# Products of zeros in TensorE's waits, and an earlier second tile, at the start of an RWKV block

## The chip, the cores and the metric

The kernel runs on one core of a Trainium2 chip. The metric is the device time of one execution in microseconds (us); lower is better. The engines of a core are TensorE (PE, matrix products into PSUM), VectorE (DVE), ScalarE (ACT), GpSimd (POOL) and SyncE (SP). Each has its own instruction stream, taken in order, and they wait for each other through semaphores. DMA transfers are issued from the queues of SP, ACT and POOL.

## The reference

The input is x with shape (2, 4096, 256). Two residual sublayers follow each other, both behind a layer normalisation without weights:

```python
x = x + attn(_layernorm(x))
x = x + ffn(_layernorm(x))
# attn: xk, xv, xr = mixes of x and x shifted by one in time
k = xk @ W_k.T;  v = xv @ W_v.T;  r = sigmoid(xr @ W_r.T)
# WKV, a scan over time with a running maximum p and numerator q
new_p = maximum(p, u + k_t)
wkv_t = (exp(p - new_p) * q + exp(u + k_t - new_p) * v_t) / (exp(p - new_p) + exp(u + k_t - new_p))
p, q  = maximum(p + w, k_t), exp(p + w - p2) * q + exp(k_t - p2) * v_t     # p2: the new p
attn = (r * wkv) @ W_o.T
# ffn, weights of -1, 0 and 1 with a scale per output
h = silu(x @ w1.T * s1) * (x @ w2.T * s2)        # 256 -> 1024
h = gelu(h @ h1.T * sh1);  h = gelu(h @ h2.T * sh2)
ffn = h @ w3.T * s3                              # 1024 -> 256
```

## The kernel before, in words

Features lie on partitions (two halves of 128, `ND` = 2), time on the free axis. Time is cut into 16 tiles of `TS` = 512 columns, 8 for each of the two sequences. Tile 0 alone is worked in two parts of 256 columns (`parts`, line 86), so that its engines can overlap, since nothing else is there to run beside it.

Every step is a generator that yields between groups of instructions: `normalise(i)` (line 260) makes the first layer normalisation, `attention(i)` (275) the mixes, the products k, v, r (`ps_k`, `ps_v`, `ps_r`, line 300), the scan (`wkv`, 204), the output product (`ps_o`, 312), the residual and the second normalisation (`layernorm`, 176), and `ffn(i)` (335) the feed-forward part. The driver at lines 387 to 402 runs tile 0's normalisation and attention, then tile 1's normalisation, and then the feed-forward of each tile with the attention of the next and the normalisation of the one after it mixed in. A scheduler then orders the instructions of each engine by priority and readiness, so the order on an engine is not simply the order of the source. A pool of buffers hands out tiles, and a new tile waits until the old one in its buffer has been read.

A layer normalisation takes the mean with a product: VectorE adds the two halves (`both`, line 182), TensorE multiplies by a matrix of 1/256 (`average`, line 167; `mean`), VectorE subtracts, ScalarE squares (line 192), VectorE adds the halves (193), TensorE multiplies again (`var`), ScalarE takes the root (196), VectorE the reciprocal (199) and the product (201). In tile 0 the averages are f32 products (line 174); in later tiles the operand is first split in a high and a low half of type fp32r (`split`, line 162; `sums`) and the product made of two.

In the feed-forward part each product is made of a high and a low half (`split_product`, line 154; lines 159 and 160 in the profile): `pa` and `pb` (first layer), `ph` (the two hidden layers), `po` (last). `pa` goes through Silu on ScalarE (`gated`, line 346), is multiplied by `pb` on VectorE (line 347) and split (`hi`, `lo`). ScalarE loads a table of functions when the kind of function changes (`ACT_TABLE_LOAD`).

PSUM pools: `ps_attn` has three buffers, `ps_sum` one, `ps_ffn` four. x is loaded on SP's and ACT's queue for tile 0 (line 93) and on POOL's for all others. POOL's queue also carries, ahead of tile 1's load, the weights w1, w2 and h1, eight copies of h2 within HBM (`h_hbm`, line 112) and w3.

Of the kernel before, what the change touches and what calls it, by code (L numbers as in the profile page):

```python
# [7 lines left out]
F32 = mybir.dt.float32  # L8
# [54 lines left out]
def split_block(ctx, tc, flags, x, vecs, w_attn, w1, w2, h1, h2, w3, out):  # L63
# [26 lines left out]

    def load_x(i):
        x_sb = xpool.tile([P, ND, TS], F32, tag="x", name="x_sb")
        for p, queue in zip(parts(i), (nc.sync, nc.scalar) if i == 0 else (nc.gpsimd,)):
            queue.dma_start(out=x_sb[:, :, p], in_=hbm(x, *tiles[i])[:, :, p])
        return x_sb

    loaded = {0: load_x(0)}
    vec = const.tile([P, NVEC], F32, name="vec")
    nc.sync.dma_start(out=vec, in_=vecs)
    wa_sb = const.tile([P, 4, ND, D], F32, name="wa_sb")  # L100
# [11 lines left out]
        nc.gpsimd.dma_start(out=h2_hbm[f], in_=h2[:, :, f * P : (f + 1) * P])  # L112
    nc.gpsimd.dma_start(out=w3_sb, in_=w3)

    mean_w = const.tile([P, P], F32, name="mean_w")
# [3 lines left out]
    eps = const.tile([P, 1], F32, name="eps")  # L119
    vector.memset(eps, LN_EPS)  # L120
    unmix = const.tile([P, 3 * ND], F32, name="unmix")
    vector.tensor_scalar(unmix, vec[:, 0 : 3 * ND], -1.0, 1.0, ALU.mult, ALU.add)

    prev = const.tile([P, ND, 1], F32, name="prev")
    log_max = const.tile([P, ND], F32, name="log_max")
    numer = const.tile([P, ND], F32, name="numer")


    pieces = []
# [24 lines left out]
    def split_product(psum, weights, src):  # L154

        n = len(src)
        for c in range(n):
            hi, lo = src[c]
            tensor.matmul(psum, weights(c), hi, start=c == 0, stop=False)  # L159
            tensor.matmul(psum, weights(c), lo, start=False, stop=c == n - 1)  # L160

    def split(hi, lo, full):

        scalar.activation(hi, full, AF.Copy)  # L164
        vector.tensor_tensor(lo, full, hi.bitcast(F32), ALU.subtract)  # L165

    def average(psum, both, busy):

        if busy:
            pieces = one.tile([P, 2, TS], F32R, tag="sums", name="sums")  # L170
            split(pieces[:, 0, :], pieces[:, 1, :], both)
            split_product(psum, lambda c: mean_wr, [(pieces[:, 0, :], pieces[:, 1, :])])
        else:
            tensor.matmul(psum, mean_w, both, start=True, stop=True)

    def layernorm(src, xc, tag, parts, busy):


        both = one.tile([P, TS], F32, tag=tag, name="both")
        mean = ps_sum.tile([P, TS], F32, tag="ps", name="mean")  # L180
        for p in parts:
            vector.tensor_tensor(both[:, p], src[:, 0, p], src[:, 1, p], ALU.add)
            average(mean[:, p], both[:, p], busy)
        for p in parts:
            for h in range(ND):
                vector.tensor_tensor(xc[:, h, p], src[:, h, p], mean[:, p], ALU.subtract)
        yield
        sq = wide.tile([P, ND, TS], F32, tag="wide", name="sq")
        var = ps_sum.tile([P, TS], F32, tag="ps", name="var")
        rstd = one.tile([P, TS], F32, tag=tag, name="rstd")  # L190
        for p in parts:
            scalar.activation(sq[:, :, p], xc[:, :, p], AF.Square)
            vector.tensor_tensor(sq[:, 0, p], sq[:, 0, p], sq[:, 1, p], ALU.add)
            average(var[:, p], sq[:, 0, p], busy)
        for p in parts:
            scalar.activation(rstd[:, p], var[:, p], AF.Sqrt, bias=eps)  # L196
        yield
        for p in parts:
            vector.reciprocal(rstd[:, p], rstd[:, p])  # L199
            for h in range(ND):  # L200
                vector.tensor_tensor(xc[:, h, p], xc[:, h, p], rstd[:, p], ALU.mult)
        yield

    def wkv(h, k, v, r, y, parts, first):

        w, u = col(DECAY, h), col(FIRST, h)

        lm = one.tile([P, TS + 1], F32, tag="lm", name="lm")
        num = one.tile([P, TS + 1], F32, tag="num", name="num")
        if first:  # L210
            vector.memset(lm[:, 0:1], LOG_ZERO)
# [14 lines left out]
        for p in parts:  # L226
            vector.tensor_tensor_scan(
                lm[:, after(p)], w.to_broadcast([P, p.stop - p.start]), k[:, p], lm[:, p.start : p.start + 1],
                ALU.add, ALU.max,
            )  # L230
            vector.scalar_tensor_tensor(sc[:, 1, p], lm[:, p], w, k[:, p], ALU.add, ALU.subtract)
            vector.tensor_scalar(sc[:, 0, p], sc[:, 1, p], NEG_CLAMP, 0.0, ALU.max, ALU.min)
            vector.tensor_scalar(sc[:, 1, p], sc[:, 1, p], 0.0, -NEG_CLAMP, ALU.max, ALU.min)
            scalar.activation(sc[:, 0, p], sc[:, 0, p], AF.Exp)
            scalar.activation(sc[:, 1, p], sc[:, 1, p], AF.Exp, scale=-1.0)
            vector.scalar_tensor_tensor(so[:, 1, p], k[:, p], u, lm[:, p], ALU.add, ALU.subtract)
            vector.tensor_scalar(so[:, 1, p], so[:, 1, p], NEG_CLAMP, -NEG_CLAMP, ALU.max, ALU.min)
        vector.tensor_copy(log_max[:, h : h + 1], lm[:, TS:])
        for p in parts:
            scalar.activation(so[:, 0, p], so[:, 1, p], AF.Sigmoid, scale=-1.0)  # L240
            scalar.activation(so[:, 1, p], so[:, 1, p], AF.Sigmoid)
            scalar.activation(r[:, p], r[:, p], AF.Sigmoid)
        yield
        for p in parts:
            vector.tensor_tensor(sc[:, 1, p], sc[:, 1, p], v[:, p], ALU.mult)
            vector.tensor_tensor_scan(
                num[:, after(p)], sc[:, 0, p], sc[:, 1, p], num[:, p.start : p.start + 1], ALU.mult, ALU.add
            )
        vector.tensor_copy(numer[:, h : h + 1], num[:, TS:])
        yield  # L250
        for p in parts:
            vector.tensor_tensor(so[:, 0, p], so[:, 0, p], num[:, p], ALU.mult)
            vector.tensor_tensor(so[:, 1, p], so[:, 1, p], v[:, p], ALU.mult)
            vector.tensor_tensor(so[:, 0, p], so[:, 0, p], so[:, 1, p], ALU.add)
            vector.tensor_tensor(y[:, h, p], so[:, 0, p], r[:, p], ALU.mult)
        yield
# [3 lines left out]
    def normalise(i):  # L260

        x_sb = loaded.pop(i)
        if i + 1 < len(tiles):
# [7 lines left out]
        yield from layernorm(x_sb, xn[:, :, 1:], "rstd1", parts(i), i > 0)  # L271
        vector.tensor_copy(prev, xn[:, :, TS:])
        normal[i] = (x_sb, xn)

    def attention(i):
# [21 lines left out]
        for h in range(ND):  # L297
            kvr = []
            for m, name in enumerate("kvr"):
                ps = ps_attn.tile([P, TS], F32, tag="pa", name="ps_" + name)  # L300
                for p in ps_of:
                    product(
                        ps[:, p],
                        lambda c, m=m: wa_sb[:, m, c, h * P : (h + 1) * P],
                        [mixed[m][:, c, p] for c in range(ND)],
                    )
                kvr.append(ps)
            yield
            yield from wkv(h, *kvr, y, ps_of, first)

        for h in range(ND):
            ps = ps_attn.tile([P, TS], F32, tag="pa", name="ps_o")
            for p in ps_of:
# [4 lines left out]
                )  # L318
                vector.tensor_tensor(x_sb[:, h, p], x_sb[:, h, p], ps[:, p], ALU.add)
        yield  # L320
        x2 = wide.tile([P, ND, TS], F32, tag="wide", name="x2")
        yield from layernorm(x_sb, x2, "rstd2", ps_of, i > 0)
# [60 lines left out]
    def run(steps):  # L383
        for _ in steps:
            pass

    normal, got = {}, {}
    run(normalise(0))
    run(attention(0))
    run(normalise(1))  # L390
    for i in range(len(tiles)):
        ahead = attention(i + 1) if i + 1 < len(tiles) else iter(())
        further = normalise(i + 2) if i + 2 < len(tiles) else iter(())
        for step, _ in enumerate(ffn(i, *got.pop(i))):

            if step >= NH:
                next(ahead, None)
            if step > 2 * NH - 2 and step % 2:
                next(further, None)
        run(ahead)  # L400
# [288 lines left out]
```

## Time and profile before

| What | us |
|---|---|
| median of 3 runs | 1613.53 (1613.01 to 1614.44) |
| the profiled execution, its own time | 1613.69 |
| its span, first to last instruction | 1611.9 |
| TensorE busy | 1571.8 |
| VectorE, ScalarE busy | 1077.4, 1014.0 |
| first `mean` product of tile 0 | 5.10 |
| first `ps_k` product | 16.85 |
| first `pa` product | 57.74 |
| first `ph` product | 77.65 |

A row of a timeline has the start in us, the time, the engine, the line, the operation, the tile written and the tiles read, the shape, the count, and in brackets the idle time before it with what ended it. f32 products of 128x256 show as two records each, so "x8" is four products. Matmuls are pipelined: of several in a row, the start-to-start distance is the cost. A row of windows has the busy time and the number of instructions of PE, PE's weight loads (PEld), DVE, ACT and POOL, then the clock granted to TensorE, the DMA share and GB/s. The mean granted clock of the core over the span is 0.993. DMA queue q10 is ACT's, q1 is SP's and q0 POOL's.

### The profile page before, as it was taken

The page shows a single profiled execution, that of the slowest core. Times are in us where ns is not written, and L with a number is a line of the kernel's source. Part 1 is how long each engine was busy: PE and PEld are TensorE (multiplying, and loading weights), DVE is VectorE, ACT ScalarE, POOL GpSimd, SP SyncE. Part 2 cuts the span into 40 slices and gives each one's busy share as a digit, 9 for nine tenths or more (in the row PEclk, how much of TensorE's full clock was granted, in tenths as well). Part 3 has the DMA queues.
Part 4 walks back from the last instruction along what each step waited for, and adds up shares of the span by engine and source line. Part 5 has one row for each costly group of instructions (what it writes and reads, how often), then busy time and mean ns, then how long its engine had stood idle before and what let it go on. Part 6 is the DMA issues. An engine that isn't in the chain of part 4 may idle for free.

```text
span 1611.9 us, 16567 instructions
## 1 busy us (share of the span) xinstructions
PE 1571.8 (98%) x6314; PEld 1189.0 (74%) x6314; DVE 1077.4 (67%) x1746; ACT 1014.0 (63%) x1351; POOL 58.4 (4%) x91
## 2 busy tenths in 40 slices
PE   4799999999999999999999999999999999999997
PEld 3577778777777777777777777777778777787786
DVE  7767667585766958668585676857668575675521
ACT  6566666766657567576666657667576666657542
POOL 2000000000000000000000000000000000000000
PEclk9899999999999999999999999999999999999999
DMA  9003122130311203113030221203112031110202
GB/s 366 26 1 105 40 79 72 33 116 15 105 53 53 92 14 118 39 52 99 19 119 27 78 72 43 96 13 102 43 53 85 7 105 40 65 59 34 91 9 72
DMA packets 36230, 109.16 MB, mean 68 GB/s; under 512 B 3632, under 2 KB 12336, under 8 KB 35504
## 3 DMA queue, kind: packets, MB, share of 16 engines
q1 hardware_dynamic: 18992, 68.45, 13.0%
q0 software_dynamic: 16880, 39.33, 7.9%
q8 instruction: 51, 0.84, 0.2%
q14 instruction: 35, 0.29, 0.1%
q10 hardware_dynamic: 272, 0.26, 0.0%
HBM read 99.64 MB, written 12.58 MB: 70 GB/s over the span
## 4 chain that ended last, share of the span: by engine, by line
PE 79%; issue 15%; DMA 3%; DVE 1%; ACT 1%; POOL 0%; POOLq 0%; ACTq 0%
PE ph L159 24%; PE ph L160 24%; PE pa L159 3%; PE pa L160 3%; PE pb L159 3%; PE pb L160 3%; PE po L159 3%; PE po L160 3%; PE ps_o L152 3%; PE ps_v L152 3%; PE ps_r L152 3%; PE ps_k L152 3%; DMA h_hbm<-in_h 1%; DMA x_sb<-in_x 1%; PE mean L159 0%
## 5 line engine op out<-in xcount | busy, mean ns | idle before, releaser
L159 PE MATMUL ph<-hi,h_sb 128*128 128x512 f32 x2048 | 817.2, 399 | 0.3 <-DMA h_sb<-h_hbm 0.3
L160 PE MATMUL ph<-lo,h_sb 128*128 128x512 f32 x2048 | 803.7, 393 | 0.0
L159 PEld LDWEIGHTS ph<-hi,h_sb 128*128 128x128 f32 x2048 | 384.6, 188 | 95.4 <-issue 7.4
L160 PEld LDWEIGHTS ph<-lo,h_sb 128*128 128x128 f32 x2048 | 385.0, 188 | 90.8 <-issue 7.2
L365 DVE TENSOR_TENSOR lo<-full,hi 128x512 fp32r<-128x512 f32 x256 | 175.3, 685 | 321.7 <-ACT full L364 321.6
L362 ACT ACTIVATE hi<-ph,vec 128x512 fp32r<-128x512 f32 x256 | 176.0, 687 | 295.5 <-PE ph L160 294.4
L364 ACT ACTIVATE full<-ph,vec 128x512 f32<-128x512 f32 x256 | 174.3, 681 | 0.0
L362 ACT ACT_TABLE_LOAD x102 | 130.9, 1283 | 1.8
L346 ACT ACTIVATE gated<-pa,vec 128x512 f32<-128x512 f32 x128 | 86.9, 683 | 63.5 <-PE pa L160 62.3
L347 DVE SCALAR_TENSOR_TENSOR gated<-pb,vec,gated 128x512 f32<-128x512 f32 x128 | 95.4, 748 | 31.3 <-PE pb L160 21.9
L199 DVE RECIPROCAL rstd<-rstd 128x512 f32<-128x512 f32 (+1 forms) x34 | 107.2, 3158 | 6.9 <-ACT rstd L196 6.9
L159 PE MATMUL pa<-x_hi,w_sb 128*128 128x512 f32 x256 | 104.5, 408 | 4.5 <-ACT x_hi L164 3.8
L160 PE MATMUL pa<-x_lo,w_sb 128*128 128x512 f32 x256 | 104.5, 408 | 0.0
L159 PE MATMUL pb<-x_hi,w_sb 128*128 128x512 f32 x256 | 102.3, 400 | 0.0
L160 PE MATMUL pb<-x_lo,w_sb 128*128 128x512 f32 x256 | 101.5, 396 | 0.0
L164 ACT ACTIVATE hi<-gated 128x512 fp32r<-128x512 f32 x128 | 80.2, 628 | 33.1 <-DVE gated L347 31.5
L159 PE MATMUL po<-hi,w_sb 128*128 128x512 f32 x256 | 99.5, 398 | 0.0
L160 PE MATMUL po<-lo,w_sb 128*128 128x512 f32 x256 | 98.6, 394 | 0.0
L165 DVE TENSOR_TENSOR lo<-gated,hi 128x512 fp32r<-128x512 f32 x128 | 87.6, 686 | 12.2 <-ACT hi L164 9.1
L289 DVE SCALAR_TENSOR_TENSOR mx<-xn,vec,mx 128x512 f32<-128x512 f32 (+1 forms) x102 | 71.3, 716 | 0.4
L152 PE MATMUL ps_k<-mx,wa_sb 128*128 128x512 f32 (+1 forms) x136 | 63.3, 584 | 5.9 <-DVE mx L289 5.6
L152 PE MATMUL ps_v<-mx,wa_sb 128*128 128x512 f32 (+1 forms) x136 | 63.0, 590 | 5.0 <-DVE num L212 5.0
(101 smaller groups left out, 1699.4 us busy)
## 6 DMA issues: line engine op xcount, KB each, us to landing
h_sb<-h_hbm SPq DMA_DIRECT2D x128, 512.0 KB, 3.3
out<-x_sb POOLq DMA_DIRECT2D x16, 512.0 KB, 3.1
raw<-in_h POOLq DMA_DIRECT2D x32, 256.0 KB, 3.1
x_sb<-in_x POOLq DMA_DIRECT2D x15, 512.0 KB, 4.1
h_sb<-in_h POOLq DMA_DIRECT2D x1, 4096.0 KB, 19.8
h_hbm<-in_h POOLq DMA_DIRECT2D x8, 512.0 KB, 23.4
w_sb<-in_w POOLq DMA_DIRECT2D x3, 1024.0 KB, 10.6
raw<-in_w POOLq DMA_DIRECT2D x12, 256.0 KB, 2.8
```

What stands on the lines that cost most here:

```text
L152: tensor.matmul(psum, weights(c), src[c], start=c == 0, stop=c == n - 1)
L159: tensor.matmul(psum, weights(c), hi, start=c == 0, stop=False)
L160: tensor.matmul(psum, weights(c), lo, start=False, stop=c == n - 1)
L164: scalar.activation(hi, full, AF.Copy)
L165: vector.tensor_tensor(lo, full, hi.bitcast(F32), ALU.subtract)
L199: vector.reciprocal(rstd[:, p], rstd[:, p])
L289: vector.scalar_tensor_tensor(mx[:, h, p], xn[:, h, p.start + 1 : p.stop + 1], vec[:, j : j + 1], mx[:, h, p], ALU.mult, ALU.add,)
L346: scalar.activation(full, pa, AF.Silu, scale=col(S1, f))
L347: vector.scalar_tensor_tensor(full, pb, col(S2, f), full, ALU.mult, ALU.mult)
L362: scalar.activation(hi, ps, AF.Gelu, scale=col(scales, f))
L364: scalar.activation(full, ps, AF.Gelu, scale=col(scales, f))
L365: vector.tensor_tensor(lo, full, hi.bitcast(F32), ALU.subtract)
```

## The change

The change touches the start of the kernel only.

- `keep_warm(n)` issues n products of a 512-column tile of zeros (`still`, fp32r) by its own first 128 columns into a PSUM tile `unread`, which nobody reads. Sixty are issued: 9 ahead of tile 0's first mean, 7 between that mean and `var`, 17 behind `var`, 6 behind the mean of tile 0's second normalisation and 21 behind its `var`. `tc.issue_after(ins)` holds the instructions of a block behind the named one on its engine.
- `layernorm` is cut in two (`column_mean` and the rest), and with `pause` it yields at more places.
- Tile 1's load goes to ACT's queue at the start. Its `both` is held behind tile 0's `sq` additions, ahead of tile 0's reciprocals; its mean is written to `ps_ffn` instead of `ps_sum`, its low half and product are held behind tile 0's second mean, its subtractions behind tile 0's last split, and the rest of its normalisation is stepped at odd steps of the first feed-forward part.
- A Sqrt of one column loads ScalarE's Sqrt table at the start, and again behind tile 0's last Sigmoid of the scan.
- In tile 0 the second half's `ps_k` and `ps_v` come from `ps_ffn` instead of `ps_attn`.

```diff
     def load_x(i):
         x_sb = xpool.tile([P, ND, TS], F32, tag="x", name="x_sb")
-        for p, queue in zip(parts(i), (nc.sync, nc.scalar) if i == 0 else (nc.gpsimd,)):
+        queues = {0: (nc.sync, nc.scalar), 1: (nc.scalar,)}.get(i, (nc.gpsimd,))
+        for p, queue in zip(parts(i), queues):
...
-    loaded = {0: load_x(0)}
+    loaded = {i: load_x(i) for i in range(2)}
...
+    def load_sqrt_table():
+        return scalar.activation(root, eps, AF.Sqrt)
+
+    load_sqrt_table()
...
+    still = hid.tile([P, TS], F32R, tag="hi", name="still")
+    zeros = tmp.tile([P, TS], F32, tag="full", name="zeros")
+    vector.memset(zeros, 0.0)
+    vector.tensor_copy(still, zeros)
+    unread = ps_ffn.tile([P, TS], F32, tag="pf", name="unread")
+
+    def keep_warm(n):
+        for _ in range(n):
+            tensor.matmul(unread, still[:, 0:P], still, start=True, stop=True)
...
+    def column_mean(src, mean, tag, parts, busy, pause=False):
+        if pause:
+            both = tmp.tile([P, TS], F32, tag="full", name="both")
         else:
-            tensor.matmul(psum, mean_w, both, start=True, stop=True)
-
-    def layernorm(src, xc, tag, parts, busy):
-        both = one.tile([P, TS], F32, tag=tag, name="both")
-        mean = ps_sum.tile([P, TS], F32, tag="ps", name="mean")
-        for p in parts:
-            vector.tensor_tensor(both[:, p], src[:, 0, p], src[:, 1, p], ALU.add)
-            average(mean[:, p], both[:, p], busy)
+            both = one.tile([P, TS], F32, tag=tag, name="both")
+        for p in parts:
+            marks["both"] = vector.tensor_tensor(both[:, p], src[:, 0, p], src[:, 1, p], ALU.add)
+            if pause:
+                yield
+            marks["mean"] = average(mean[:, p], both[:, p], busy)
+
+    def layernorm(src, mean, xc, tag, parts, busy, pause=False):
...
+        if pause:
+            yield
         for p in parts:
             scalar.activation(rstd[:, p], var[:, p], AF.Sqrt, bias=eps)
...
+        pool, tag = (ps_ffn, "pf") if i == 1 else (ps_sum, "ps")
+        mean = pool.tile([P, TS], F32, tag=tag, name="mean")
+        yield from column_mean(x_sb, mean, "rstd1", parts(i), i > 0, i == 1)
+        if i == 1:
+            yield
...
-                ps = ps_attn.tile([P, TS], F32, tag="pa", name="ps_" + name)
+                pool, tag = (ps_ffn, "pf") if i == 0 and h and name != "r" else (ps_attn, "pa")
+                ps = pool.tile([P, TS], F32, tag=tag, name="ps_" + name)
...
+        if i == 0:
+            with tc.issue_after(marks["sigmoid"].ins):
+                load_sqrt_table()
...
-    run(normalise(0))
-    run(attention(0))
-    run(normalise(1))
+    here, second = normalise(0), normalise(1)
+    keep_warm(9)
+    next(here)
+    with tc.issue_after(marks["mean"].ins):
+        keep_warm(7)
+    next(here)
+    with tc.issue_after(marks["var"].ins):
+        keep_warm(17)
+    with tc.issue_after(marks["sq"].ins):
+        next(second)
+    with tc.issue_after(marks["both"].ins):
+        run(here)
+    here = attention(0)
+    for _ in range(3 + 4 * ND + 2):
+        next(here)
+    with tc.issue_after(marks["mean"].ins):
+        keep_warm(6)
+    with tc.issue_after(marks["both"].ins):
+        next(second)
+    next(here)
+    with tc.issue_after(marks["var"].ins):
+        keep_warm(21)
+    run(here)
+    with tc.issue_after(marks["split"].ins):
+        next(second)
     for i in range(len(tiles)):
...
+            if i == 0 and step % 2:
+                next(second, None)
```

More of the change, by code (lines that the diff above doesn't have):

```diff
@@ L113, in split_block @@
     nc.gpsimd.dma_start(out=w3_sb, in_=w3)
+    eps = const.tile([P, 1], F32, name="eps")
+    vector.memset(eps, LN_EPS)
+    root = const.tile([P, 1], F32, name="root")
+    def load_sqrt_table():
+        return scalar.activation(root, eps, AF.Sqrt)
+    load_sqrt_table()
     mean_w = const.tile([P, P], F32, name="mean_w")
@@ L118, in split_block @@
     scalar.activation(mean_wr, mean_w, AF.Copy)
-    eps = const.tile([P, 1], F32, name="eps")
-    vector.memset(eps, LN_EPS)
     unmix = const.tile([P, 3 * ND], F32, name="unmix")
@@ L159, in split_product @@
             tensor.matmul(psum, weights(c), hi, start=c == 0, stop=False)
-            tensor.matmul(psum, weights(c), lo, start=False, stop=c == n - 1)
+            last = tensor.matmul(psum, weights(c), lo, start=False, stop=c == n - 1)
+        return last
     def split(hi, lo, full):
-        scalar.activation(hi, full, AF.Copy)
-        vector.tensor_tensor(lo, full, hi.bitcast(F32), ALU.subtract)
+        marks["high"] = scalar.activation(hi, full, AF.Copy)
+        marks["split"] = vector.tensor_tensor(lo, full, hi.bitcast(F32), ALU.subtract)
     def average(psum, both, busy):
@@ L171, in average @@
             split(pieces[:, 0, :], pieces[:, 1, :], both)
-            split_product(psum, lambda c: mean_wr, [(pieces[:, 0, :], pieces[:, 1, :])])
-        else:
-            tensor.matmul(psum, mean_w, both, start=True, stop=True)
-    def layernorm(src, xc, tag, parts, busy):
-        both = one.tile([P, TS], F32, tag=tag, name="both")
-        mean = ps_sum.tile([P, TS], F32, tag="ps", name="mean")
+            return split_product(psum, lambda c: mean_wr, [(pieces[:, 0, :], pieces[:, 1, :])])
+        return tensor.matmul(psum, mean_w, both, start=True, stop=True)
+    def column_mean(src, mean, tag, parts, busy, pause=False):
+        if pause:
+            both = tmp.tile([P, TS], F32, tag="full", name="both")
+        else:
+            both = one.tile([P, TS], F32, tag=tag, name="both")
         for p in parts:
-            vector.tensor_tensor(both[:, p], src[:, 0, p], src[:, 1, p], ALU.add)
-            average(mean[:, p], both[:, p], busy)
+            marks["both"] = vector.tensor_tensor(both[:, p], src[:, 0, p], src[:, 1, p], ALU.add)
[3 more added lines that the diff above has]
+    def layernorm(src, mean, xc, tag, parts, busy, pause=False):
         for p in parts:
@@ L192, in layernorm @@
             scalar.activation(sq[:, :, p], xc[:, :, p], AF.Square)
-            vector.tensor_tensor(sq[:, 0, p], sq[:, 0, p], sq[:, 1, p], ALU.add)
-            average(var[:, p], sq[:, 0, p], busy)
+            marks["sq"] = vector.tensor_tensor(sq[:, 0, p], sq[:, 0, p], sq[:, 1, p], ALU.add)
+            marks["var"] = average(var[:, p], sq[:, 0, p], busy)
+        if pause:
+            yield
         for p in parts:
@@ L240, in wkv @@
             scalar.activation(so[:, 0, p], so[:, 1, p], AF.Sigmoid, scale=-1.0)
-            scalar.activation(so[:, 1, p], so[:, 1, p], AF.Sigmoid)
+            marks["sigmoid"] = scalar.activation(so[:, 1, p], so[:, 1, p], AF.Sigmoid)
             scalar.activation(r[:, p], r[:, p], AF.Sigmoid)
@@ L262, in normalise @@
         x_sb = loaded.pop(i)
-        if i + 1 < len(tiles):
+        if i + 1 < len(tiles) and i > 0:
             loaded[i + 1] = load_x(i + 1)
+        pool, tag = (ps_ffn, "pf") if i == 1 else (ps_sum, "ps")
[3 more added lines that the diff above has]
+            yield
         xn = one.tile([P, ND, TS + 1], F32, tag="xn", name="xn")
@@ L270, in normalise @@
             vector.tensor_copy(xn[:, :, 0:1], prev)
-        yield from layernorm(x_sb, xn[:, :, 1:], "rstd1", parts(i), i > 0)
+        yield from layernorm(x_sb, mean, xn[:, :, 1:], "rstd1", parts(i), i > 0, i == 0)
         vector.tensor_copy(prev, xn[:, :, TS:])
@@ L320, in attention @@
         yield
+        if i == 0:
+            with tc.issue_after(marks["sigmoid"].ins):
+                load_sqrt_table()
+        mean = ps_sum.tile([P, TS], F32, tag="ps", name="mean")
+        yield from column_mean(x_sb, mean, "rstd2", ps_of, i > 0)
         x2 = wide.tile([P, ND, TS], F32, tag="wide", name="x2")
-        yield from layernorm(x_sb, x2, "rstd2", ps_of, i > 0)
+        yield from layernorm(x_sb, mean, x2, "rstd2", ps_of, i > 0, i == 0)
         x2_hi = one.tile([P, ND, TS], F32R, tag="x2_hi", name="x2_hi")
@@ L385, in run @@
             pass
[L387 to L390 removed]
+    normal, got, marks = {}, {}, {}
+    here, second = normalise(0), normalise(1)
[23 more added lines that the diff above has]
+        next(second)
     for i in range(len(tiles)):
```

## The prediction

> **What bounds the kernel now.** I read the page's busy shares first, then TensorE's waits after 76 us, then the first 80 us in windows of 5 us, then each engine's timeline there.
>
> ```profile
> PE 1571.8 (98%) x6314; PEld 1189.0 (74%) x6314; DVE 1077.4 (67%) x1746; ACT 1014.0 (63%) x1351; POOL 58.4 (4%) x91
> ...
> PE ph L159 <- DMA h_sb<-h_hbm: 0.3, 1, 0.3
> ```
>
> The second line is all that TensorE (PE) waits for between 76 us and the end. From the first `ph` product at 77.65 us PE runs without a gap, and the change leaves the products behind that point as they are, so each microsecond by which that product comes earlier is a microsecond of the result. The question is the first 77.65 us.
>
> ```profile
> 10.00:15.00 5.00, 1.21 (x3) 0.43 (x2) 3.25 (x2) 1.43 (x3) 0.89 (x2) 1.00 1.12 469
> ...
> 25.00:30.00 5.00, 2.00 (x9) 1.44 (x8) 4.60 (x14) 4.93 (x9) 1.46 (x2) 1.00 2.01 327
> 30.00:35.00 5.00, 2.68 (x7) 2.16 (x8) 4.87 (x16) 4.52 (x8) 0.00 (x0) 0.76 1.40 365
> ...
> 55.00:60.00 5.00, 2.26 (x5) 1.43 (x6) 4.42 (x9) 1.80 (x3) 0.00 (x0) 0.50 0.00 0
> 60.00:65.00 5.00, 5.00 (x17) 3.91 (x16) 2.51 (x4) 4.46 (x7) 0.00 (x0) 0.67 0.02 5
> ```
>
> Columns: window, busy PE, PEld, DVE, ACT, POOL, then the granted clock. VectorE (DVE) and ScalarE (ACT) set the pace from 15 to 41 us; a faster PE gains nothing there. In the two normalisations of tile 0 (5 to 15 and 46 to 58 us) the engines hand work to each other, so PE's latency counts, and PE runs at clock 0.50 from 49.7 to 63.2 us.
>
> ```profile
> 16.85 3.78 PE L152 MATMUL ps_k<-mx,wa_sb 128*128 128x256 f32 x8 [5.64 <-DVE mx L289]
> 25.29 1.99 PE L152 MATMUL ps_k<-mx,wa_sb 128*128 128x256 f32 x8 [0.28 <-DVE so L236]
> 49.76 2.08 PE L174 MATMUL var<-sq,mean_w 128*128 128x256 f32 x4 [1.96 <-DVE sq L193]
> ...
> 42.72 0.69 DVE L182 TENSOR_TENSOR both<-x_sb 128x512 f32<-128x512 f32 x1 [1.78 <-DMA x_sb<-in_x]
> 43.33 0.42 DVE L254 TENSOR_TENSOR so<-so 128x256 f32<-128x256 f32 x1
> ```
>
> The same eight records take 3.78 cold and 1.99 warm: 0.43 us each against 0.215, two records to an f32 product, so 0.86 against 0.43. A 128x512 product is 0.43 cold, 0.234 warm. The early rows are cold although the clock column reads 1.00 there: durations decide. Line 42.72: the second tile's sum heads VectorE's queue, waits 1.78 for its DMA, and tile 0's L254 and L255 are stuck behind it.
>
> **The change, part by part.** Times are span times; the order on each engine is that of the changed program.
>
> (1) *First mean, nine zero products ahead.* The zeros need two small memsets, one of 512 columns (about 0.5, from mean_w's 0.17 for 128) and a copy (0.48, from a 512-column TENSOR_SCALAR): PE starts at 2.05. Nine cold ones are 0.6+8x0.427=4.0, so `mean` starts at 6.05, not 5.10. When does the clock come up? Rows: the burst from 32.32 was cold until 36.0 (3.7 us), those from 16.85 and 57.74 for 5.5 us. [...] The seven zeros behind (1.6 to 3.0) fit in the 2 us before `var`. `var` is then warm: its second half ends 0.63 after its operand, not 1.4 (11.2-9.8): -0.75. Net -0.27: first reciprocal 11.5, not 11.76. The Sqrt table loaded early saves nothing more here (9.31 to 10.59 lay beside `var`), but would have bound a warm `var`.
>
> (2) *Second tile's load on ACT's queue and its sum ahead of the reciprocals.* It no longer stalls VectorE at 41: -1.78-0.61=-2.4 there. Its new place is VectorE's idle time from 9.74 to 11.76, if the 512 KB have landed; behind it wait rstd's reciprocals, and all of tile 0 behind those. It starts when ACT's half of tile 0 is through, at about 4.7, against w_attn on SP and w1 on POOL.
>
> ```profile
> q0 software_dynamic: 45, 0.37, 93.5%
> q10 hardware_dynamic: 58, 0.05, 14.6%
> q1 hardware_dynamic: 101, 0.03, 13.7%
> ```
>
> That is 4 to 5 us (packets, MB, share): small packets pass 159 to 45 large ones, so not one for one. One for one, 16 packets of 2 KB per engine would land at about 13.9 (w_attn's eight turns at 0.74, then eight at 0.41; 8 KB are 0.935x16/45=0.33 us of an engine); by bytes at about 8.5; at three for one, the nearest row, 9.6. [...] I take 9.6, no stall; from 10.8 on it costs its lateness, 3.1 at the worst. The second issue on ACT's queue (0.47, the row of the first) delays only its first table load, which has until 10 us; POOL's queue has one issue less. The rest of that sum, `sums` (0.69), goes from 44.66 to beside tile 0's second mean product, which is as long; uncovered it would cost 0.69.
>
> (3) *Seventeen zeros behind `var`:* 4.0 warm, ended at 14.9 while ps_k's operand comes at 16.6. They cost nothing and gain nothing: VectorE is busy with mx until the first scan, t0=20.87 (21.14-0.27).
>
> (4) *WKV.* The new order does r's first sigmoid before the Exps: seven table loads of 1.28 instead of eight. It does not show, as VectorE and the chain Exp, Sigmoid, multiply bind in turn. Adding the rows' durations in the new order, the first half of y's second block ends at t0+19.35, the second at t0+20.15 (before, without the stall, about +20.5).
>
> (5) *What is late next: ps_o.* k and v of the second half now go straight through free PSUM buffers (gone: 5.04 us of waiting at 32.3, which nothing needed). But those products at 32 to 37.5 were what warmed the clock before ps_o. Now PE is idle from about 33 to t0+19.4, and no zeros stand there. [...] Working it through: the subtraction behind the second mean is at t0+24.2 all warm, t0+25.6 to +26.9 cold; I take +26.3, i.e. 47.2 against 47.84. The 2.4 of (2) shrink to under 0.4 here; with (1), 0.65.
>
> (6) *Second variance and first FFN layer.* Six zeros and one real product (1.64 warm) fit in the 1.92 to `var`; its table is loaded earlier. `var` warm is -0.8 (2.08 to about 1.3 with its second half last). The 21 zeros take 4.9 of the 5.9 to pa. pa starts at 56.3, not 57.74: -1.4 so far. Then twelve products at 0.234 instead of 0.43 (-2.5 for PE alone), but ScalarE has 16.7 us here (eight gated at 0.65, eight hi at 0.62, the second tile's sq, sums and rstd 2.4, three loads 3.9):
>
> ```profile
> 64.75 1.28 ACT L196 ACT_TABLE_LOAD   x1
> ...
> 66.76 3.35 DVE L199 RECIPROCAL rstd<-rstd 128x512 f32<-128x512 f32 x1 [0.88 <-ACT rstd L196]
> ...
> 69.30 0.50 PE L159 MATMUL pa<-x_hi,w_sb 128*128 128x512 f32 x1 [0.68 <-ACT gated L346]
> ```
>
> The Sqrt load and the reciprocal are what hold PE here, through the gated queued behind them. The new order puts two more gated in front of both. Walking it: gated3 done at pa+8.1, load, rstd +10.1, two hi, Silu load, gated4 +13.3 (PE waits 1.5), reciprocal to +13.5, last pb at +16.85 (PE waits 0.65), first ph at pa+17.8 against 19.9: -2.1.
>
> Sum: 0.65+0.8+2.1=3.55, against the profiled execution (1613.69, that is span 1611.9 plus 1.8 around it). The median is 0.16 lower: 1613.53-3.55=1610.0.
>
> **Rivals.**
> - *Tile 1 lands late.* For: three rings share 420 GB/s. Against: the packet counts. From 10.8 us on every microsecond passes to the end; at 12 to 13.9 the result is 1611.2 to 1613.1.
> - *The clock holds in ps_o* (or ScalarE's stage packs better). For: a window with 1.56 busy (39.4 to 42.8) didn't lower it. Against: an empty one did at 32.7, and here PE is empty for over 7 us. It gives 2.1 more: 1607.9, down to 1606.5 with an early rise in (1) and ScalarE's stage 0.6 tighter.
> - *Zeros don't raise the clock*, the slower side. [...] If zeros didn't count, nine, seven and seventeen are 14 us cold: var ends 1.6 late, ps_k starts at 19.8 instead of 16.6 and k, v, r at 0.86 reach ScalarE's first sigmoid some 3 late; the 21 take 9.0 where 5.9 are free, 3 late. With the stall saved (2.4): about +6, 1619.5. It decides once a zero product takes over 0.29 us (4.9/17, or 5.9/21).
>
> **How the numbers follow.** Main 0.66, with its own range 1608.4 to 1611.6 (rise of the clock +-0.9, first layer +-0.8, landing); late tile 0.15; clock holds 0.12; zeros don't count 0.07. A measurement of this kernel tells about 0.2% from no change, 3.2 us: faster means under 1610.3. Main splits 0.38 faster, 0.28 same; late tile 0.01 and 0.14; clock holds 0.12 faster; zeros 0.06 slower, 0.01 same. Faster 0.51, same 0.43, slower 0.06. The range takes in the late tile and the clock rival: 1606.5 to 1613.2.
>
> **What would show it.** Right: `var` rows at about 1.3 us; no DMA ahead of `both`; ps_o's first rows at 0.43 a record; clock 1.00 from pa on; VectorE idle near 10 us; first ph near 74.1. Wrong: `both` of tile 1 waiting past 10.8, zero products at 0.43 after 9 us, pa waiting for zeros, or PE gaps behind the first ph.

## The result, and the profile after

The changed kernel takes 1607.40 us (median of 6 runs, 1606.32 to 1607.79) against 1613.49 (6 runs): a ratio of 0.9962, 95% interval 0.9952 to 0.9972, that is 6.1 us or 0.38% faster. 1610.0 was predicted, with a range of 1606.5 to 1613.2 and, for the main case alone, 1608.4 to 1611.6. The direction was right; the gain came out 2.5 us larger than the sum.

The profiled execution took 1607.79 (span 1606.0), 5.90 less than that of before. S is VectorE's subtraction behind tile 0's second mean.

| stretch (us) | before | sum of the prediction | after |
|---|---|---|---|
| start to S | 47.84 | -0.65 | 46.87 (-0.97) |
| S to first `pa` | 9.90 | -0.8 | 9.19 (-0.71) |
| first `pa` to first `ph` | 19.91 | -2.1 | 17.21 (-2.70) |
| first `ph` to the end of the span | 1534.25 | 0 | 1532.73 (-1.52) |
| together | 1611.9 | -3.55 | 1606.0 (-5.90) |

The busy shares of the page, and TensorE's timeline at the start (start, duration, engine, line, operation, tiles, shape, count, idle time before it):

```profile
PE 1578.3 (98%) x6374; PEld 1196.9 (75%) x6374; DVE 1078.0 (67%) x1748; ACT 1011.1 (63%) x1351; POOL 58.0 (4%) x90
```

```profile
2.09 4.21 PE L145 MATMUL unread<-still 128*128 128x512 f32 x9 [2.09 <-DVE num L240]
6.09 1.41 PE L193 MATMUL mean<-both,mean_w 128*128 128x256 f32 x4
7.15 1.97 PE L145 MATMUL unread<-still 128*128 128x512 f32 x7
9.47 1.36 PE L193 MATMUL var<-sq,mean_w 128*128 128x256 f32 x4 [0.35 <-DVE sq L219]
10.48 4.25 PE L145 MATMUL unread<-still 128*128 128x512 f32 x17
16.47 2.43 PE L171 MATMUL ps_k<-mx,wa_sb 128*128 128x256 f32 x10 [1.74 <-DVE mx L323]
...
31.40 2.08 PE L171 MATMUL ps_o<-y,wa_sb 128*128 128x256 f32 x4 [4.07 <-DVE y L283]
40.27 4.90 PE L171 MATMUL ps_o<-y,wa_sb 128*128 128x256 f32 x12 [6.79 <-DVE y L283]
```

TensorE's busy time grows by 6.5 us for the sixty products, and the span is 5.9 shorter all the same. The nine start cold (4.21 for nine), the four records of `mean` take 1.41 instead of 2.07, as the clock rises in the middle of them (at 6.85), and the seven (1.97) and `var` (1.36 instead of 2.07) are warm: in this execution the clock came up and stayed up on products of zeros. The seventeen end 1.74 ahead of `ps_k`. `ps_o` is cold from its first pair on (four records in 2.08): the clock was lost in the 4.07 of idle time ahead of that pair (0.50 granted from 30.75 on), and another 6.79 follow. VectorE's timeline of after, around the two places where work was moved, and the issue of tile 1's load:

```profile
9.99 0.68 DVE L203 TENSOR_TENSOR both<-x_sb 128x512 f32<-128x512 f32 x1
11.38 3.37 DVE L227 RECIPROCAL rstd<-rstd 128x256 f32<-128x256 f32 x2 [0.70 <-ACT rstd L224]
...
46.87 1.41 DVE L212 TENSOR_TENSOR x<-x_sb,mean 128x256 f32<-128x256 f32 x4 [0.19 <-PE mean L193]
```

```profile
x_sb<-in_x ACTq DMA_DIRECT2D x1, 512.0 KB, 4.7
```

Tile 1's sum has no wait ahead of it, so its load was there. Issued at 1.25, it landed 4.7 later, at 6.0; the prediction took 9.6. The windows of after (busy PE, PEld, DVE, ACT, POOL, then the granted clock) show where the clock is missing and that it holds from 45 us on, where before had 0.50 from 49.7 to 63.3:

```profile
35.00:40.00 5.00, 0.00 (x0) 0.00 (x0) 4.33 (x12) 4.91 (x8) 0.00 (x0) 0.50 1.85 364
40.00:45.00 5.00, 4.73 (x13) 3.65 (x13) 2.69 (x8) 0.68 (x2) 0.00 (x0) 0.56 0.55 212
45.00:50.00 5.00, 4.11 (x17) 2.59 (x16) 3.71 (x9) 1.26 (x2) 0.00 (x0) 1.00 0.00 0
...
55.00:60.00 5.00, 3.94 (x17) 3.12 (x18) 3.73 (x8) 3.76 (x6) 0.00 (x0) 1.00 0.01 2
```

TensorE's waits in the first feed-forward layer, and the first `ph`, in after:

```profile
56.06 0.50 PE L178 MATMUL pa<-x_hi,w_sb 128*128 128x512 f32 x1 [1.11 <-ACT x_hi L184]
...
67.62 0.40 PE L179 MATMUL pb<-x_lo,w_sb 128*128 128x512 f32 x1
68.70 0.50 PE L178 MATMUL pa<-x_hi,w_sb 128*128 128x512 f32 x1 [0.69 <-ACT gated L387]
...
69.50 0.40 PE L179 MATMUL pa<-x_lo,w_sb 128*128 128x512 f32 x1
70.37 0.50 PE L178 MATMUL pb<-x_hi,w_sb 128*128 128x512 f32 x1 [0.47 <-ACT gated L387]
...
73.27 0.40 PE L178 MATMUL ph<-hi,h_sb 128*128 128x512 f32 x1
```

The two waits that step (6) named are there. Their cost is the start-to-start distance less the 0.233 of a product: 0.85 (67.62 to 68.70) and 0.64 (69.50 to 70.37), where it had 1.5 and 0.65.

### The profile page after: what moved, and what is told of

It is laid out like the page before. It is cut to its first block, busy times and chain, and to the rows that moved or that the text cites. A ratio compares the mean times of both kernels' runs of the same rounds, so it can differ in the third digit from the quotient of the medians.

```text
span 1606.0 us, 16687 instructions
## 1 busy us (share of the span) xinstructions
PE 1578.3 (98%) x6374; PEld 1196.9 (75%) x6374; DVE 1078.0 (67%) x1748; ACT 1011.1 (63%) x1351; POOL 58.0 (4%) x90
## 4 chain that ended last, share of the span: by engine, by line
PE 81%; issue 15%; DVE 2%; ACT 1%; POOL 0%; POOLq 0%; DVEq 0%; ACTq 0%
PE ph L179 24%; PE ph L178 24%; PE pa L178 3%; PE pb L178 3%; PE pb L179 3%; PE pa L179 3%; PE ps_o L171 3%; PE po L179 3%; PE po L178 3%; PE ps_r L171 3%; PE ps_v L171 3%; PE ps_k L171 3%; DVE rstd L227 1%; PE mean L178 0%; PE var L178 0%
## 5 line engine op out<-in xcount | busy, mean ns | idle before, releaser
L171 PE MATMUL ps_o<-y,wa_sb 128*128 128x512 f32 (+1 forms) x136 | 61.1, 594 | 10.9 <-DVE y L283 10.9
L262 ACT ACTIVATE sc<-sc 128x512 f32<-128x512 f32 (+1 forms) x34 | 20.7, 609 | 68.4 <-DVE sc L260 68.3
```

The source lines that it names most:

```text
L171: tensor.matmul(psum, weights(c), src[c], start=c == 0, stop=c == n - 1)
```

## The experiments

All are edits of the changed kernel, but for the one that starts from the kernel before. They ran in groups on several chips, each beside runs of the kernel before; so ratios are compared across groups, times only within one. Columns from the profile: VectorE's first scan, S, first `pa`, first `ph`.

| run | median us | ratio to before, 95% | scan | S | `pa` | `ph` |
|---|---|---|---|---|---|---|
| before | 1613.49 | 1 | 21.14 | 47.84 | 57.74 | 77.65 |
| changed | 1607.40 | 0.9962 (0.9952 to 0.9972) | 20.75 | 46.87 | 56.06 | 73.27 |
| changed, second chip (c_after) | 1608.37 | 0.9964 (0.9950 to 0.9977) | 20.03 | 45.87 | 55.06 | 72.28 |
| changed, third chip (c2_after) | 1607.81 | 0.9959 (0.9945 to 0.9972) | 20.75 | 46.87 | 56.06 | 73.27 |
| no zeros | 1611.38 | 0.9979 (0.9973 to 0.9986) | 21.09 | 45.83 | 55.02 | 74.75 |
| early load alone | 1611.34 | 0.9980 (0.9973 to 0.9987) | 21.17 | 47.00 | 56.25 | 75.89 |
| no nine | 1608.57 | 0.9964 (0.9950 to 0.9977) | 21.00 | 46.97 | 56.17 | 73.39 |
| no 21 | 1610.34 | 0.9981 (0.9972 to 0.9990) | 19.93 | 45.72 | 54.91 | 74.60 |
| tile 1's rest in one piece | 1609.11 | 0.9971 (0.9960 to 0.9982) | 19.88 | 45.49 | 54.96 | 72.58 |
| 37 more zeros | 1607.74 | 0.9959 (0.9945 to 0.9972) | 20.64 | 46.55 | 55.74 | 72.96 |
| 47 more, until `ps_o` | 1606.69 | 0.9955 (0.9942 to 0.9969) | 21.25 | 45.67 | 54.86 | 72.09 |
| no 17 | 1607.57 | 0.9953 (0.9939 to 0.9966) | 20.90 | 46.68 | 55.87 | 73.09 |
| no 17, zeros until `ps_o` | 1605.37 | 0.9941 (0.9928 to 0.9955) | 20.20 | 43.92 | 53.12 | 70.33 |
| the same without the nine | 1605.41 | 0.9943 (0.9929 to 0.9957) | 21.40 | 45.05 | 54.25 | 71.46 |

**No zeros at all.** All else of the change stays.

```diff
-        for _ in range(n):
+        for _ in range(0):
```

> The changed kernel without any zero product; all else stays. Theory (sum of steps, each with its own cover): the first normalisation loses nothing, since the mean starts at about 4.7 instead of 6.1 and its two cold products take back what the warm ones gained, so the first reciprocal stays within 0.3 us of 11.4. The cold products k, v and r make ScalarE's first sigmoid late, worth 0.5 us; the second variance is cold, 0.75 us; the first feed-forward layer starts cold, about 1.3 us. Sum 2.5 us more than the changed kernel, 1609.9. Rival (the early load and the new order are the whole gain, zeros are idle work): 1607.4. Rival (the clock is the whole gain): back to 1613.

Half of the gain is left: 3.1 us under the kernel before on its chip. `pa` even comes a microsecond earlier than in the changed kernel (55.02 against 56.06), and all of the zeros' worth lies behind it: `pa` to `ph` takes 19.73 instead of 17.21. That the part up to `pa` is faster in this profile was a surprise; the run without the 17 takes it up.

**The early load alone**, on the kernel before: tile 1 on ACT's queue, nothing else.

```diff
+        queues = {0: (nc.sync, nc.scalar), 1: (nc.scalar,)}.get(i, (nc.gpsimd,))
-    loaded = {0: load_x(0)}
+    loaded = {i: load_x(i) for i in range(2)}
```

> The kernel before with one part of the change: the second tile's load goes to ACT's queue at the start. Theory: the wait of 1.78 us ahead of VectorE's sum of the second tile is gone, and its sum and split move into the stretch in which VectorE is busy all the time, so that the gain is 1.8 us at most: 1611.7. The products k and v of the second half still warm the clock ahead of ps_o. Rival (the load is the whole gain): 1607.4. Rival (the load lands no earlier): 1613.5.

First `ph` is 1.76 earlier than before, as expected, and the time (1611.34) lies within 0.4 of the expected 1611.7; the 3.15 by medians is against a chip on which the kernel before took 1614.49. `pa` to `ph` is 19.64: the load does nothing there. Beside it, on the same chip, the kernel without zeros took 1611.38: without the zeros, the early load is all of the gain that the times show, although the profile without zeros has its first `ph` 1.1 earlier.

The load itself holds a surprise. Its row, and the packets of ACT's queue from 6 to 13 us:

```profile
x_sb<-in_x ACTq DMA_DIRECT2D x1, 512.0 KB, 12.2
```

```profile
q10 hardware_dynamic: 12, 0.02, 0.9%
```

The same load, issued at 1.25 as in after, landed at 13.4 here and not at 6.0. That does no harm in this kernel, whose sum of tile 1 comes at 21.88; in the changed kernel it would have held up tile 0's reciprocals. The load is 256 packets of 2 KB. In after all of them had started by 5.6, when 22 packets of 8 KB had gone out on the other two queues (the first at 5.1 and 5.4). Here twelve were left at 6 us, and these start one by one, first 0.70 and later 0.40 us apart, between the 8 KB packets. In all twelve profiles of the changed kernel and its variants the load landed between 6.0 and 6.5; what gives them the lead was not isolated.

**Without the nine, and without the 21.**

```diff
-    keep_warm(9)
```

> The changed kernel without the nine zero products ahead of the first mean. Theory: what they hold up (0.95 us) and what they gain in the clock are nearly equal, so 1607.4 within 0.5 us; the mean starts at about 4.7 and the seven zeros behind it are cold and end at about 9.5. Rival (they are what raises the clock for the first variance): the seven cold zeros overrun the variance by 1.2 us and it is cold itself, 1609.

```diff
-        keep_warm(21)
+        keep_warm(0)
```

> The changed kernel without the 21 zero products behind the second variance. PE then has nothing between var (ends about 50) and pa (56.1). [...] Rival A, these zeros do nothing because the layer is ScalarE's throughout: 0 +-0.3. Rival B, PE's loss counts in full: +2.5. [...]

The nine are worth nothing that the times show. The 21 are worth 2.0 by medians and 2.3 at the first `ph`. `pa` to `ph` is 19.69 against 17.22 in the changed kernel on the same chip, 2.47 more. TensorE's timeline without the 21:

```profile
54.91 0.80 PE L178 MATMUL pa<-x_hi,w_sb 128*128 128x512 f32 x1 [5.90 <-ACT x_hi L184]
55.63 0.79 PE L179 MATMUL pa<-x_lo,w_sb 128*128 128x512 f32 x1
...
59.64 0.44 PE L178 MATMUL pa<-x_hi,w_sb 128*128 128x512 f32 x1
59.92 0.39 PE L179 MATMUL pa<-x_lo,w_sb 128*128 128x512 f32 x1
...
74.60 0.40 PE L178 MATMUL ph<-hi,h_sb 128*128 128x512 f32 x1
```

Ten products take 54.91 to 59.64, that is 4.73; ten warm ones take 2.46 in the changed kernel beside it. PE's loss of 2.3 arrives at `ph` in full: rival B, and not the author's estimate by step (6), in which ScalarE hides a part (1.0 to 1.8 later at `ph`).

By their ratios the early load is worth 0.20% and the 21 zeros 0.17% (each +-0.1), of 0.38% for the whole change. So these two are the gain, as far as the times can tell; the seven and the six zeros, the early Sqrt loads and the PSUM buffers were not run on their own.

**Tile 1's rest in one piece**, ahead of the layer and not in steps of it.

```diff
-    with tc.issue_after(marks["split"].ins):
-        next(second)
+    run(second)
...
-            if i == 0 and step % 2:
-                next(second, None)
```

> The changed kernel with the rest of the second tile's normalisation issued in one piece ahead of the first FFN layer, not in pieces at every second step of it. All zeros and the early load stay. Theory of step (6): the Sqrt table load and the reciprocal of 3.35 us then stand ahead of gated products that were before them in the changed order, and hold pa and pb up: first ph 1.0 to 2.0 later (74.3 to 75.3), the time longer by as much. Rival: with a warm pa the order inside the layer no longer matters, as ScalarE has the same work in both orders: 0 +-0.3. If both this and the kernel without the 21 zeros lose about what they save together (2.7 from pa to first ph), the two parts add up; if each alone loses nearly all of it, they need one another.

`pa` to `ph` is 17.62 against 17.22: 0.40 longer, near the rival; the time is 0.7 longer, within the intervals. ScalarE's rows of this run show the Sqrt load and root ahead of all but the first `gated`, earlier than in before (64.75), and yet PE makes nearly all of it up:

```profile
57.11 0.69 ACT L387 ACTIVATE gated<-pa,vec 128x512 f32<-128x512 f32 x1 [0.29 <-PE pa L179]
57.81 1.28 ACT L224 ACT_TABLE_LOAD   x1
59.11 0.69 ACT L224 ACTIVATE rstd<-var,eps 128x512 f32<-128x512 f32 x1
```

With a cold `pa` the order is worth next to nothing: 19.73 (no zeros, new order) against 19.64 (load alone, old order) and 19.91 (before). So of the 2.70 in this layer some 2.3 to 2.5 are the clock and 0.2 to 0.4 the order.

**The changed kernel again, twice**, as the yardstick.

> The changed kernel once more, beside the other three on the same chip: the yardstick for them, and a second profile of the stretch from the first ph product to the last product. That stretch was 1524.5 us in the profile of the kernel before, 1524.4 and 1524.7 in the kernels without zeros and with the early load alone, 1523.0 in the changed kernel and 1523.3 and 1523.4 in the two others that keep the 21 zeros, the finer order and the early load. If the 1.5 us belong to the kernel, the stretch is 1523.0 +-0.3 here; if they belong to that one execution or to a chip, it may be anywhere from 1523 to 1525. First ph at 73.3 either way; ratio to the kernel before 0.996.

> The changed kernel again, as the yardstick on the chip of the next one and as another draw of when the clock rises: ratio to the kernel before 0.996, first reciprocal between 10.4 and 11.9 as in the eight profiles with nine zeros so far (mean 11.1).

The start differs between executions of one program. TensorE's timeline of the second chip's run, to be read against that of after above:

```profile
2.09 3.82 PE L145 MATMUL unread<-still 128*128 128x512 f32 x9 [2.09 <-DVE num L240]
5.75 1.02 PE L193 MATMUL mean<-both,mean_w 128*128 128x256 f32 x4
6.42 1.98 PE L145 MATMUL unread<-still 128*128 128x512 f32 x7
```

Here the clock rises at 5.3, within the nine and before any other product, and not at 6.9; `ps_k` comes 0.73 earlier and S 1.0 earlier. Over the nine profiles with nine zeros the rise lay between 5.0 and 8.0 us (from the granted clock), and the first reciprocal between 10.49 and 11.87, mean 11.10; before it was 11.76, and without the nine 11.61 and 12.02.

First `ph` to the last product: 1523.0 in after, 1523.34 and 1523.27 in these two, so about 1523.2 belongs to the kernel; 1524.50 before and 1524.69 with the early load alone.

**Zeros in WKV.** The clock is lost in the idle time ahead of `ps_o`; 15 zeros stand behind the second head's last `ps_r`, and 22, then 32 in a second kernel that is otherwise the same, behind the first pair of `ps_o` products.

```diff
+            if c == 0:
+                marks["first"] = last
+        marks["product"] = last
...
+                if p.start == 0:
+                    marks["ps_o"] = marks["first"]
...
-    for _ in range(3 + 4 * ND + 2):
+    for _ in range(3 + 4 + 1):
         next(here)
+    with tc.issue_after(marks["product"].ins):
+        keep_warm(15)
+    for _ in range(3 + 1):
+        next(here)
+    with tc.issue_after(marks["ps_o"].ins):
+        keep_warm(22)
+    next(here)
```

> The changed kernel with 37 zero products more in the idle time of tile 0's scan: 15 behind the last product r and 22 behind the first two ps_o products. Theory (ps_o runs cold because PE stood idle before it): its rows go from 0.43 to 0.215 us a record, the subtraction behind the second mean comes 1.9 us earlier, and the end with it: 1605.5. Rival (VectorE's additions set that stretch anyway, or the zeros hold up ps_o): 1607.4 or more.

> The changed kernel with 47 more zero products, in the idle time of PE before ps_o: 15 behind the last r product of the second head and 32 (not 22) behind the first pair of ps_o products. The 22 ended at 37.6, left PE idle for 2.7 us and the clock fell; 32 end at about 39.9, just ahead of ps_o's next operand at 40.2. Theory of step (5): the clock holds, the twelve ps_o records are warm (0.215 to 0.22 each instead of 0.43), the subtraction behind the second mean comes at 44.8 to 45.3 instead of 46.9, and the time is 1.6 to 2.1 shorter than that of the changed kernel (ratio to the kernel before about 0.995). Rival A: the chain there is set by VectorE's x_sb additions, and a warm ps_o gains under 0.5. Rival B: the zeros run late and hold ps_o up: longer by 0.3 to 1. Rival C: the lead is lost again at the Sqrt table or at the reciprocal of the second normalisation, so that the subtraction comes early but pa at 55.7 or later.

TensorE in the run with 22:

```profile
32.20 5.38 PE L145 MATMUL unread<-still 128*128 128x512 f32 x22
40.28 4.56 PE L171 MATMUL ps_o<-y,wa_sb 128*128 128x256 f32 x12 [2.71 <-DVE y L286]
```

and with 32:

```profile
32.66 7.64 PE L145 MATMUL unread<-still 128*128 128x512 f32 x32
40.76 3.21 PE L171 MATMUL ps_o<-y,wa_sb 128*128 128x256 f32 x12 [0.45 <-DVE y L286]
```

22 were too few: with 2.71 of idle time ahead of `ps_o` the clock fell at 40.75, just after `ps_o` began, and the expected gain did not come. With 32 it holds: twelve records take 3.21 instead of 4.3 to 4.9, and from the first scan to S it is 24.42, against 25.84 to 26.12 in the changed kernel. Part of this was hidden by an unlucky start (first scan at 21.25, 1.2 later than in the changed kernel's run beside it), so the absolute S is only 0.2 earlier there; by medians the run is 1.7 faster than the changed kernel beside it (1606.45 to 1607.14 against 1606.51 to 1608.82). That is the theory of step (5).

**Without the 17.**

```diff
-        keep_warm(17)
+        keep_warm(0)
```

> The changed kernel without the 17 zero products behind the first variance. Step (3) said of them: they cost nothing and gain nothing. ps_k, ps_v and ps_r of the first head then start cold, which VectorE hides (first scan 9.37 behind the first reciprocal, in the kernel with no zeros and in the changed one alike). But the order written for VectorE and ScalarE in WKV is another without them, that of the kernel with no zeros: two Exps before the first sigmoid. There ps_o's second operand came 18.5 behind the first scan, in the changed kernel 19.5 to 19.8. Theory: the 17 zeros cost 1.0 through that order, so first ph is 1.0 earlier and the time 0.7 to 1.3 shorter than that of the changed kernel (ratio to the kernel before 0.9955 to 0.996). Rival A, step (3) as put: 0 +-0.3. Rival B, the cold ps_k does count, or the order costs what it saves: longer by 0.3 to 1.

The order changes as said. ScalarE's timeline in after:

```profile
19.97 1.28 ACT L270 ACT_TABLE_LOAD   x1
22.39 0.37 ACT L270 ACTIVATE ps_r<-ps_r 128x256 f32<-128x256 f32 x1 [1.14 <-PE ps_r L171]
22.77 1.28 ACT L262 ACT_TABLE_LOAD   x1
...
29.24 1.28 ACT L262 ACT_TABLE_LOAD   x1
31.92 0.42 ACT L262 ACTIVATE sc<-sc 128x256 f32<-128x256 f32 x1 [1.40 <-DVE sc L260]
```

and in the kernel without zeros, whose order in WKV this one has:

```profile
20.30 1.28 ACT L262 ACT_TABLE_LOAD   x1
22.97 0.42 ACT L262 ACTIVATE sc<-sc 128x256 f32<-128x256 f32 x1 [1.39 <-DVE sc L260]
```

With the 17, r's sigmoid goes first: ScalarE loads a table for one instruction, and waits 1.40 for VectorE at 31.92. (That the scheduler counts `ps_r` as early behind zeros is argued, not shown.) Without them `ps_o`'s second operand comes 18.50 behind the first scan (39.40 less 20.90), not 19.52. But the microsecond is nearly lost again at once, as `ps_o` is cold for longer (this run, then that without the 17 and with zeros until `ps_o`):

```profile
39.40 5.57 PE L171 MATMUL ps_o<-y,wa_sb 128*128 128x256 f32 x12 [6.35 <-DVE y L283]
```

```profile
32.24 6.07 PE L145 MATMUL unread<-still 128*128 128x512 f32 x25
38.77 3.44 PE L171 MATMUL ps_o<-y,wa_sb 128*128 128x256 f32 x12 [0.47 <-DVE y L286]
```

In the first the clock rose only 5.3 behind `ps_o`'s start, so S is at 25.78 behind the scan, 0.3 better than in after. In the kernel without zeros, with the same order, it rose 3.2 behind it and S is at 24.74: that microsecond is the luck of one execution. By its ratio the run looks 0.1% faster, by its median not at all; the intervals overlap, so for the time this run alone is inconclusive. The next one settles it: it has 5 zeros behind the last `ps_r` and 25 behind the first pair of `ps_o`.

> The kernel with zeros until ps_o, without the 17 zero products and with the later ones sized for the faster order: 5 behind the last r product of the second head, 25 behind the first pair of ps_o products. If the gain of the order (1.0) and that of a warm ps_o (1.4 to 1.7 from ps_o's second start to the subtraction behind the second mean: 4.9 there, 6.1 to 6.6 in the changed kernel) add up, the subtraction comes 23.4 to 23.7 behind the first scan (24.4 with the warm ps_o alone, 25.8 to 26.1 in the changed kernel), first ph at about 70.7 to 71.5, and the time is 2.0 to 2.8 shorter than that of the changed kernel, ratio to the kernel before 0.9945 to 0.995. Rival A: they don't add up, as in this order VectorE has x_sb's additions between the halves of y: 1.0 to 1.6 shorter. Rival B: the clock falls in the 1.4 us behind the last r product or in front of ps_o; then as the kernel without the 17 alone.

With the clock held, both gains add up: S comes 23.72 behind the first scan, 2.1 to 2.4 better than in the changed kernel, first `ph` at 70.33, and 1605.37 us, ratio 0.9941. Last, the same without the nine, beside the changed kernel on one chip:

> The kernel without the 17 zeros and with a warm ps_o, now also without the nine zeros ahead of the first mean: the order of all else is unchanged. With the nine, the clock rose 3.1 to 5.8 us behind the first zero in eight profiles, and the first reciprocal came at 10.5 to 11.9, mean 11.1; without them it came at 11.6. Step (1) gave nine and seven together 0.27. By these profiles the nine are worth about 0.5 on average: then this is about 0.5 slower than with them, and 1.5 to 2.0 faster than the changed kernel on this chip (first reciprocal 11.6, first ph at 71.1). Rival: the nine are worth nothing or less, as 0.95 of real work is held up by them: then 2.0 to 2.5 faster than the changed kernel.

1605.41 against 1607.81 there: 2.4 faster than the changed kernel, 8.6 faster than the kernel before. Its ratio is that of the version with the nine within 0.0002, so the nine show no worth in the time; its start (first reciprocal 12.02) was the latest of all profiles, S 23.65 behind the scan. Both versions beat the two kernels of the case.

## Why the prediction was right and wrong

- **(1) First mean.** Right that `var` is warm behind the zeros (1.36 against 2.07), and nearly right in size. `mean` started at 6.09 (6.05 said), the first reciprocal came at 11.38 (11.5), and the clock rose at another time from one execution to the next (5.3 on the second chip, 6.9 in after). The -0.27, and with it the 0.65 of the sum, holds +0.5 for a late rise of the clock, and the range +-0.9 for its time: no run shows these two terms. What the runs show is a rise 2.9 to 5.9 behind the first zero, in the nine profiles with nine zeros. Mean gain 0.66 for nine and seven, 0.38 in the first profile, 0.27 predicted.
- **(2) Tile 1.** Right that its sum would not wait (`both` at 9.99), wrong in when the load lands: 6.0, where it took 9.6 and its earliest estimate, by bytes, was 8.5. The late rival did not happen here, but the run with the early load alone shows it at 13.4, close to the 13.9 of one packet for one, and its last twelve packets start one by one, 0.70 and 0.40 apart where that sum had 0.74 and 0.41. The three small packets to one large that the prediction took are not what made it early: in after the small ones had simply started ahead of nearly all the large ones, by 5.6. For the prediction, that is luck.
- **(3) The seventeen.** Right that they end ahead of `ps_k`'s operand, wrong that they cost nothing: they changed the planned order in WKV by 1.0 us. As step (4) had worked with the order that contains this cost, the sum was not hurt; it missed a gain, not a loss.
- **(4) WKV and (5) `ps_o`.** Right, though TensorE's idle time begins earlier than the 33 that it said: the last `ps_r` starts at 25.21, and the first pair of `ps_o` is already cold. Second half of `y` at 19.46 and 20.25 behind the scan (19.35 and 20.15), S at 26.12 (26.3, within 25.6 to 26.9), all warm 24.42 (24.2). How long `ps_o` stays cold is a term of that range, and so of the 0.65, that no run shows as it was put: from the start of the twelve records to the rise it was 4.1 in after (40.27 to 44.40), 3.2 in the kernel without zeros and 5.3 without the 17. The rival "the clock holds" fell in its first half: `ps_o` was cold.
- **(6) First feed-forward layer.** This is the step that was mis-sized: 2.1 said, 2.70 measured. `pa` at 56.06 (56.3) and `var` warm at 1.36 were right. The claim that failed is "but ScalarE has 16.7 us here": by it ScalarE would hide part of PE's 2.5, and the order around the Sqrt load would be what pays. The run without the 21 shows PE's loss arriving in full (2.47), and the run in one piece shows the order paying 0.40. The layer has 66 products at 0.233, 15.4 of the 17.2: PE was the bound once warm. Of the two waits left, the second cost 0.64 as said (0.65), the first 0.85 and not 1.5: ScalarE had done the fourth `gated` at pa+7.5, not at +8.1, and kept that lead through the Sqrt load and the root (+9.55, not +10.1). That is the 0.6 between the sum and the measurement.
- **Behind the first `ph`.** The opening sentence "each microsecond by which that product comes earlier is a microsecond of the result" left out a term: 1.52, 1.33 and 1.12 in the three profiles of the changed kernel. From the first `ph` to the last product it is 1524.5 and 1524.7 in before and with the early load alone, 1523.0 to 1523.6 in eleven profiles of the changed kernel and its variants, and 1524.4 in the variant without zeros, of which one distance of 1.22 between two `ph` products, 1.0 over the usual, is a wait for `h_sb`. About 0.3 is in the mean products of the later tiles, most of which stand 0.63 instead of 0.66 ahead of their second halves; 0 to 0.4 is a wait for `h_sb`, 0.3 in before and none in after; the rest is spread over thousands of products. It goes with the changed program, and not with the order in the first layer alone (1523.5 in the run in one piece); why was not isolated.
- **Zeros don't raise the clock** fell: `var` (1.36), `ps_k` (ten records in 2.43) and `pa` (ten products in 2.46 on the second chip) are all warm behind zeros, and on the second chip the clock rose, at 5.3, when nothing but zeros had run.

The measured 1607.40 is below the main case's own range (1608.4 to 1611.6). It lies inside the whole range because that had room for "the clock holds in ps_o (or ScalarE's stage packs better)": the first half of this did not happen, the second is worth 0.6, and 1.5 came from behind the first `ph`, for a reason that no case named. That the sum of these falls there is luck.

## What to carry to other kernels

Before letting another engine hide part of a gain, add up the work of the engine that gets faster: here 66 products at 0.233 are 15.4 of 17.2 us, so TensorE bounds the layer and its gain arrives in full. Size filler by how much of each stretch of time it fills, not by the length of the gap that it leaves: 1.96 us of idle time lost the clock in before, and 1.91 did not in the run without the 17. In these profiles a warm clock held behind every stretch of 3.41 us with at least 1.50 us of products and fell behind every one with at most 1.40, and where the stretches lay differed between executions of one program; so filler spread over a whole wait is the safer choice here, an estimate from these numbers. Where a planner orders the engines, filler on one of them can reorder the others; compare the orders before reading a run without it as the worth of the filler.

## What the runs showed of the hardware

- In the first 85 us of all fourteen profiles the changes of the granted clock lie multiples of 3.41 us apart within a profile (in before 22.37, 32.61, 36.02, 49.67, 63.33, in after 6.85, 30.75, 44.40). Each profile was cut into stretches of 3.41 that line up with these changes. TensorE's busy time in a stretch, as the windows count it, then sorts all stretches of these profiles without an exception: a warm clock fell behind every one with at most 1.40 of busy time and held behind every one with at least 1.50; a cold one rose behind every one with at least 2.90 and stayed cold behind every one with at most 2.59. The four stretches nearest to the borders are one of before (it holds), one without the 17 (it falls), one without the 17 and the nine (stays cold) and one of the run in one piece (rises):

```profile
25.78:29.19 3.41, 1.50 (x7) 0.97 (x6) 3.04 (x9) 3.35 (x6) 1.46 (x2) 1.00 2.17 316
```

```profile
31.06:34.47 3.41, 1.40 (x4) 0.59 (x4) 3.27 (x10) 3.33 (x7) 0.00 (x0) 1.00 1.16 385
```

```profile
4.20:7.61 3.41, 2.59 (x6) 2.13 (x7) 1.44 (x5) 0.00 (x0) 2.80 (x4) 1.00 1.08 422
```

```profile
1.58:4.99 3.41, 2.90 (x7) 2.33 (x8) 0.96 (x6) 1.69 (x3) 3.41 (x6) 1.00 0.86 265
```

- The length of a gap does not sort them. Before lost the clock at 49.67 with a gap of 1.96 us, as the stretch from 46.26 had 1.31 of busy time; the run with 22 zeros lost it with 0.70 in the stretch from 37.34. Where the stretches lay differed between executions of one program: in three profiles of the changed kernel the clock rose at 5.3 once and at 6.9 twice, and the first `ph` came at 72.28 and twice at 73.27.
- The kernel before took 1611.8 to 1616.4 over 73 executions beside the experiments, on four chips; those with a mean granted clock of 0.991 averaged 1615.6 (24), those with 0.993 1613.6 (21).
- The time of one load differed between runs. The 512 KB of tile 1, issued at 1.25 on ACT's queue, took 4.7 us to land in after and 12.2 with the early load alone, where its last twelve packets started one by one between the 8 KB packets of two other queues. From 4 to 5 in after ACT's queue moved 202 packets, SP's 43 and POOL's none: such a count does not tell how the queues share the engines when all of them have work.
